# Conv sequence on one core: layer 1's weight steps in three slots, and layer 2's second packed weights made during layer 1

## The chip, the cores and the metric

The kernel runs on one core of a Trainium2 chip. The metric is the device time of one execution in microseconds, as the median of several runs. One execution before was also profiled, and all views below come from it.

## The reference, cut to what matters

Four layers run one after another on a tensor of 16 images, 256 channels and 28 x 28 pixels.

```python
# layer 0: sign of x, 3x3 convolution with sign weights, batch norm, + x
y  = conv3x3(sign(x), sign(w0)) * mean(|w0|);  x = batchnorm(y) + x
# layer 1: 3x3 convolution of signs with real weights, gates, 1x1 convolution, gates
y  = prelu(bn(conv3x3(sign(x), clip(a_w)))); y = bn(gate(y) * y * prelu(x)) + prelu(x)
u  = prelu(bn(conv1x1(sign(y), clip(f_w)))); x = bn(gate(u) * u) + y
# layer 2: two 3x3 convolutions with sign weights, batch norms between and after
h  = prelu(sf1 * conv3x3(sign(batchnorm(x)), sign(w1)), a1)     # sf1 = mean(|w1|)
h  = prelu(sf2 * conv3x3(sign(batchnorm(h)), sign(w2)), a2)     # sf2 = mean(|w2|)
x  = prelu(batchnorm(h) + x, a3)
# layer 3: attention over the 784 pixels of each image, + x
```

The batch norms are over all images. So each convolution with a batch norm behind it has to be finished, statistics included, before the next stage can take its first sign.

## The kernel before, in words

Channels lie on the 128 partitions, in two halves `k`. The work is in stages, and the batch norms part them: layer 0 (up to about 120 us), layer 1 (to about 495 us), the first convolution of layer 2 (to about 604 us, called 2a here), the second (to about 711 us, called 2b), and layer 3.

**Packed sign weights.** Weights of +1 and -1 for two output halves are packed in one fp16 number (`packed_weights`, six chunks). `sign_weights` makes them in six steps: a DMA of 384 KB brings a chunk `st`, ScalarE takes its sign (`sg`, L266) and VectorE packs two halves (`wpk`, L267). `w0` is for layer 0, `w2a` for 2a, and `w2b` for 2b.

**Weight sums.** `weight_sums` brings weights by rows and lets ScalarE sum |w| (L285) and |sign w| (L288), six steps for each layer. `add_up` (L294, L295) ends them on VectorE.

**A step** is a pair of functions: `load` issues the DMA on the SP queue, `work` issues the ScalarE and VectorE work and returns a function for what is to be issued later. `load_ahead(steps, 2)` issues each load two steps before its work.

**`sign_layer`** is the convolution loop of layer 0, 2a and 2b. Within it the order of PE, ScalarE, VectorE and SP is the order in which the program writes it. For each block (an image in layer 0, half an image in layer 2) it issues the matmuls (`products`, L340), the signs of the next image (`sign_image`: L451 in layer 0, L1047 in layer 2), the statistics of the block before (`post`), then one step for each half image, and last the unpacking of this block (`apart`). Unpacking takes the packed sums out of PSUM: ScalarE rounds (L351, L352), VectorE subtracts (L354), and PSUM has three buffers. `post` in layer 0 is `bn_stats` (L588). In layer 2 it is a PReLU and `bn_stats` for each of two channel halves (L1081, L1083), and a square on ScalarE (L1086). The loop that hands out the steps is

```python
for p in range(len(pieces(block))):
    if late:
        late()
    step = steps.pop(0) if first_part(block) + p >= 2 and steps else None
    late = step() if step else None
apart(j)
```

After half image 26 the statistics so far are gathered (`moments.gather`, L167, L168).

**Layer 0's steps** come in rounds of four slots, that is two images, six rounds: `w1_step` (layer 1's weights for one tap row), an empty slot, a step of layer 0's weight sums, a step of `w2a`. `w1_step` clips the weights on VectorE (L501), forms three sums of taps (`asm`, L134), and splits four results in a high part on ScalarE (L510) and a low part on VectorE (L511). The loads share three buffers, tag `x2`.

**Layer 1** is `iteration(b)`, one for each image, about 22 us. Its PE, VectorE and ScalarE order is written out by hand; the order of SP there is the scheduler's. The 3x3 convolution is done as row transforms (`vs`, L134) and matmuls at L686, with sums taken out by L707, L717 and L726; the 1x1 convolution is L796. At the end of iterations 1 to 12 stands one step of the weight sums of `w2a` and `w2b` (`sums12`).

**Between stages** `keep_busy(n)` issues matmuls on zeros (L432). At the end of 2a there are 30 of them, at the end of 2b 45.

**In 2a** the steps of `w2b` take slot 6 and every fourth slot after it, up to slot 26, counted in half images; their loads are issued two steps ahead, the first two at slot 2.

Of the kernel before, what the change touches and what calls it, by code (L numbers as in the profile page):

```python
# [40 lines left out]
B = 16  # L41
# [42 lines left out]
def forward(ctx: ExitStack, tc: tile.TileContext, d: dict, out: bass.AP, careful: bool):  # L84
# [48 lines left out]
    def tt(o, a, b, op):  # L133
        V.tensor_tensor(o, a, b, op)  # L134
        return o
# [112 lines left out]
    def load_ahead(steps, n, now=True):  # L248

        for s in steps[:n] if now else ():  # L250
            s.load()
        return [lambda s=s, t=t: (s.work(), t.load() if t else None)[0] for s, t in zip(steps, steps[n:] + [None] * n)]
# [20 lines left out]
    def weight_sums(room, src, total, at):  # L273


        parts = const.tile([P, 2, 3], F32, name=f"abs_{at}")
        sts = {}

        def load(mo, q):
            st = sts[mo, q] = room()  # L280
            nc.sync.dma_start(out=st, in_=src[mo, :, q * PIECE:(q + 1) * PIECE])

        def work(mo, q):
            st = sts.pop((mo, q))
            A.activation(st, st, AF.Abs, accum_out=parts[:, mo, q:q + 1])  # L285
            if not careful:
                n = at + 3 * mo + q
                A.activation(st, st, AF.Sign, accum_out=nonzero[:, n:n + 1])  # L288
            if (mo, q) == (1, 2):
                return add_up  # L290
            return lambda: None

        def add_up():
            V.tensor_reduce(total, parts, AX.X, ALU.add)  # L294
            V.tensor_scalar(total, total, 1.0 / K9, None, ALU.mult)  # L295

        return [Step(lambda c=c: load(*c), lambda c=c: work(*c)) for c in ((mo, q) for mo in range(2) for q in range(3))]
# [122 lines left out]
    with tc.tile_pool(name="ps_conv", bufs=3, space=PSUM) as psc, \  # L420
# [13 lines left out]
        with tc.tile_pool(name="ph1", bufs=1) as ph:  # L434
# [55 lines left out]
            fw = [ph.tile([P, 2, 256], FR, name=f"fw_{i}") for i in range(2)]  # L490

            def w1_step(k, c):
                sts = []

                def load():
                    sts.append(xpool.tile([P, 3, 256], F32, tag="x2", name="st", bufs=3))
                    nc.sync.dma_start(out=sts[0], in_=d["w1"][k, :, c::3, :])

                def work():
                    st = sts[0]  # L500
                    V.tensor_scalar(st, st, -1.0, 1.0, ALU.max, ALU.min)  # L501
                    t = ph.tile([P, 3, 256], F32, tag="rn", name="asm", bufs=2)
                    a, s, m = (t[:, i, :] for i in range(3))
                    tt(a, st[:, 0, :], st[:, 2, :], ALU.add)
                    tt(s, a, st[:, 1, :], ALU.add)
                    tt(m, a, st[:, 1, :], ALU.subtract)

                    for u, (w, f) in enumerate(((st[:, 0, :], 1.0), (s, 0.5), (m, 0.5), (st[:, 2, :], -1.0))):
                        hi, lo = (x[:, k, c, u, :] for x in w1)
                        A.activation(hi, w, AF.Copy, scale=f)  # L510
                        V.scalar_tensor_tensor(lo, w, f, hi.bitcast(F32), ALU.mult, ALU.subtract)  # L511

                return Step(load, work)

            def fw_step():
                sts = []

                def load():
                    sts.append(xpool.tile([P, 3, 256], F32, tag="x2", name="stf", bufs=3))
                    nc.sync.dma_start(out=sts[0][:, 0:2, :], in_=d["fw"])  # L520

                return Step(load, lambda: split2(fw, sts[0][:, 0:2, :]))
# [45 lines left out]
                    nc.sync.dma_start(out=w_2[64 + 32 * g:65 + 32 * g], in_=d[f"seb2_{q}"])  # L568
                tt(mix_c[:, 1], pv("f_scale"), c2, ALU.mult)

            steps = [w1_step(k, c) for k in range(2) for c in range(3)] + [fw_step()]
            w2a = packed_weights(wpool, tag="wa2")

            def room_sums():
                return xpool.tile([P, PIECE], F32, tag="x2", name="sts", bufs=3)

            signs2, sums0 = sign_weights(xpool, w2a, d["w2a"], ("x2", 3), tmp=ph), weight_sums(room_sums, d["w0_rows"], sf0, 0)
            steps = [s for three in zip(steps, sums0, signs2) for s in three] + steps[6:]
            steps = load_ahead(steps, 2)
            steps[19:19] = [constants]  # L580
            for i in range(6):
                steps[4 * i + 1:4 * i + 1] = [None]

            def post0(block, ab):
                b, r0, rows = block
# [37 lines left out]
            def room_sums():  # L623
                return ph.tile([P, PIECE], F32, tag="sts", name="sts", bufs=2)

            sums12 = weight_sums(room_sums, d["w2a_rows"], sf1, 6) + weight_sums(room_sums, d["w2b_rows"], sf2, 12)

            sums = {}

            def sums_of(t):  # L630
                if t not in sums:
# [207 lines left out]
            def iteration(b):  # L839


                ahead, one, two = b + 1 < B, b >= 1, b >= 2
                if b + 2 < B:
                    xs[b + 2] = None
                    load_x(b + 2, True)
                if b < len(sums12):
                    sums12[b].load()
                for i, u in enumerate((1, 2)):
                    conv_pair(b, 0, i, u)
                if two:  # L850
                    unit_u(b - 2, 0)
                if two:
                    unit_u(b - 2, 1)
                if ahead:
                    enter(b + 1, 0, sc0)
                if one:
                    prelu_y(b - 1, 1)
                if ahead:
                    enter(b + 1, 1, sc0)
                    sign1(b + 1, 0)  # L860
                if two:
                    unit_b(b - 2, 0)
                    unit_b(b - 2, 1)
                sum_pair_a(b, 0)
                conv_pair(b, 0, 0, 0)
                h = hidden_a(b, hidden_x(b)) if one else None
                if ahead:
                    residual_a(b + 1, 0)
                    sign1(b + 1, 1)
                sum_pair_b(b, 0)  # L870
                if one:
                    h = hidden_b(b, h)
                if ahead:
                    residual_a(b + 1, 1)
                    residual_b(b + 1, 0)
                    transform(b + 1, 1)
                    residual_b(b + 1, 1)
                conv_pair(b, 0, 1, 3)
                rows_out(b, 0)
                if one:  # L880
                    g = gates(h)
                else:
                    gate_bias()
                if ahead:
                    transform(b + 1, 2)
                if one:
                    for k in range(2):
                        branch1_a(b - 1, k, g[:, 0])
                for i, u in enumerate((1, 2)):
                    conv_pair(b, 1, i, u)  # L890
                if one:
                    branch1_b(b - 1, 0)
                    branch1_c(b - 1, 0)
                    branch1_b(b - 1, 1)
                prelu_y(b, 0)
                if two:
                    branch2(b - 2, 0, g[:, 1])
                sum_pair_a(b, 1)
                sum_pair_b(b, 1)
                if one:  # L900
                    branch1_c(b - 1, 1)
                if two:
                    branch2(b - 2, 1, g[:, 1])
                    for k in range(2):
                        squares2(b - 2, k)
                if one and b <= len(sums12):
                    sums12[b - 1].work()()
                if ahead:
                    transform(b + 1, 0)
                    transform(b + 1, 3)  # L910
                    for i, u in enumerate((0, 3)):
                        conv_pair(b, 1, i, u)
                    rows_out(b, 1)
                    if one:
                        conv1x1(b - 1)
                else:
                    conv1x1(b - 1)
                    for k in range(2):
                        unit_u(b - 1, k)
                        unit_b(b - 1, k)  # L920
                    for i, u in enumerate((0, 3)):
                        conv_pair(b, 1, i, u)
                    px = hidden_x(B)
                    rows_out(b, 1)
                    prelu_y(b, 1)
                    return px
# [101 lines left out]
        pt = [ppool.tile([P, 2, N], F32, name=f"p_{b}") for b in range(B)]  # L1028

        with tc.tile_pool(name="ph2", bufs=1) as ph:  # L1030
            w2b = packed_weights(ph, tag="wb")
            fpads = sign_pads(ph, "fpads")

            def temp(tag):
# [68 lines left out]
                    while last_squares:  # L1103
                        last_squares.pop(0)()

            steps = sign_weights(xpool, w2b, d["w2b"], ("x2", 3), tmp=ph)

            def first_loads(some=steps[:2]):
                for s in some:
                    s.load()  # L1110

            steps = [first_loads, None] + [t for s in load_ahead(steps, 2, now=False) for t in (None, None, s, None)]
            mom = block_moments("l2b", HALVES)
            sign_layer(fpads, w2a, temp, room2, sign2a, post2(order, pv("a1"), mom, doubts[:, 2 * NB:3 * NB]), steps, mom, HALVES)
            late_squares()
# [601 lines left out]
```

## Time and profile before

| | us |
|---|---|
| median of 3 runs (996.99 to 997.12) | 997.11 |
| the profiled execution's own time | 997.06 |
| its span, first to last instruction | 995.0 |
| PE busy in the span | 961.2 |
| VectorE busy | 799.2 |
| ScalarE busy | 676.3 |
| first matmul of 2a / first matmul of 2b | 495.11 / 605.14 |

The profiled time is 2.06 us more than the span, for what lies around it, and 0.05 us below the median. A busy share is an average over stages with different limits, so it doesn't say what a stage waits for. In the timeline a row is: start, duration, engine, line, operation, tiles, shape, count, and in brackets the idle time before it with what ended it. A row can merge several instructions of one kind. In the table by windows the columns are busy time and count for each engine, then the granted TensorE clock (1.00 is full), the share of DMA time and GB/s.

### The profile page before, as it was taken

How to read it: one execution, taken by the hardware profiler on the slowest of the kernel's cores; microseconds unless marked ns; L12 is line 12 of the kernel's file. 1: busy time of each engine (PE TensorE's matmuls, PEld its weight loads, DVE VectorE, ACT ScalarE, POOL GpSimd, SP SyncE). 2: the span in 40 equal slices, each digit the busy share in tenths (PEclk: the TensorE clock that was granted, in tenths of full speed). 3: DMA queues.
4: the chain of work that ended last, by engine and by line, in shares of the span. 5: the costliest groups of instructions: out<-in, count | busy, mean ns of one | idle time of the engine just before them, and what ended most of it. 6: DMA issues, size and time to landing. Idle time of an engine off the chain costs nothing. (4 is left out here: it accounts for less than half of the span.)

```text
span 995.0 us, 14743 instructions
## 1 busy us (share of the span) xinstructions
PE 961.2 (97%) x5609; PEld 663.4 (67%) x5615; DVE 799.2 (80%) x1416; ACT 676.3 (68%) x1135; POOL 140.9 (14%) x149
## 2 busy tenths in 40 slices
PE   7999899999999999999999998999999999999996
PEld 3555499999999999999555554555444444444442
DVE  4666988999899899996789996999848677777765
ACT  6787436676676666664688876888676767676652
POOL 3000100000000000000100000000053535353521
PEclk9999999999999999999999999999999999999999
DMA  9977512323333322101293100000033343434312
GB/s 346 329 267 251 192 32 80 97 97 120 117 122 120 104 98 82 65 33 64 105 349 130 54 13 1 1 1 1 1 66 62 101 99 97 105 91 113 83 65 101
DMA packets 26949, 105.82 MB, mean 106 GB/s; under 512 B 3491, under 2 KB 7269, under 8 KB 26869
## 3 DMA queue, kind: packets, MB, share of 16 engines
q1 hardware_dynamic: 20948, 73.44, 21.2%
q0 software_dynamic: 5632, 30.54, 11.3%
q8 instruction: 46, 0.75, 0.3%
q10 hardware_dynamic: 288, 0.80, 0.2%
q14 instruction: 35, 0.28, 0.1%
HBM read 72.67 MB, written 32.11 MB: 105 GB/s over the span
## 5 line engine op out<-in xcount | busy, mean ns | idle before, releaser
L340 PE MATMUL cv<-fpads,wpk 128*128 128x392 f16 (+1 forms) x1746 | 297.6, 332 | 14.3 <-ACT fpads L451 5.2
L686 PE MATMUL cv<-vs,w 128*128 128x392 f32 x1536 | 303.0, 355 | 2.8 <-DVE vs L134 2.8
L686 PEld LDWEIGHTS cv<-vs,w 128*128 128x128 f32 x1536 | 288.6, 191 | 4.9 <-issue 3.2
L340 PEld LDWEIGHTS <-wpk 128*128 128x128 f16 x1746 | 169.5, 98 | 142.8 <-issue 13.8
L1296 ACT ACTIVATE es<-sc 128x784 f32<-128x784 f32 x112 | 87.3, 822 | 41.7 <-PE sc L1292 41.7
L1292 PE MATMUL sc<-q,keyswa 64*128 64x392 f32 x448 | 90.0, 513 | 0.9 <-ACT es L1296 0.9
L1081 DVE SCALAR_TENSOR_TENSOR p<-ab,vec 128x392 f32<-128x392 f32 x128 | 79.1, 618 | 2.3
L1313 PE MATMUL av<-es,v 128*64 128x392 f32 x448 | 80.8, 500 | 0.0
L1292 PEld LDWEIGHTS sc<-q,keyswa 64*128 64x128 f32 x448 | 38.9, 186 | 43.9 <-issue 17.1
L1306 POOL TENSOR_TENSOR sum<-sum,es 128x784 f32<-128x784 f32 x32 | 67.2, 2099 | 3.1 <-ACT es L1296 0.6
L134 DVE TENSOR_TENSOR vs<-pad 128x840 fp32r<-128x840 bf16 (+1 forms) x66 | 64.5, 1001 | 0.1
L1313 PEld LDWEIGHTS av<-es,v 128*64 128x64 f32 x448 | 29.4, 136 | 47.3 <-issue 47.0
L824 POOL DMA_DIRECT2D x2d<-x x16 | 8.6, 537 | 359.7 <-DVE x L818 295.1
L1280 DVE COPY keyswa<-mi 64x392 f32<-64x392 f32 x31 | 16.3, 564 | 52.6 <-ACT q L1276 52.5
L707 ACT ACTIVATE t<-cv,c_bn,s_bn 128x392 f32<-128x392 f32 x32 | 21.7, 678 | 49.9 <-PE cv L686 49.9
L351 ACT ACTIVATE t<-cv,rounding 128x392 f32<-128x392 f32 (+2 forms) x82 | 51.4, 627 | 5.2 <-PE cv L340 3.4
L1086 ACT ACTIVATE t<-ab 128x392 f32<-128x392 f32 x64 | 33.5, 523 | 30.0 <-DVE ab L354 30.0
L354 DVE SCALAR_TENSOR_TENSOR ab<-ab,cv 128x392 f32<-128x392 f32 x64 | 35.4, 554 | 20.9 <-ACT ab L352 20.0
L796 PE MATMUL cv<-z,fw 128*128 128x392 f32 x256 | 49.1, 343 | 1.0 <-ACT z L788 0.9
L796 PEld LDWEIGHTS cv<-z,fw 128*128 128x128 f32 x256 | 45.9, 188 | 2.2 <-ACT z L788 2.2
L1269 PE MATMUL mi<-p,wqk 128*128 128x392 f32 x124 | 45.3, 507 | 0.3 <-DVE p L1256 0.3
L1304 POOL TENSOR_TENSOR sum<-es 128x784 f32<-128x784 f32 x16 | 30.0, 1877 | 91.0 <-ACT es L1296 91.0
(284 smaller groups left out, 1459.3 us busy)
## 6 DMA issues: line engine op xcount, KB each, us to landing
xs<-in_x_dram SPq DMA_DIRECT2D x30, 784.0 KB, 4.8
x2d<-x POOLq DMA_DIRECT2D x16, 784.0 KB, 3.6
out_dram<-p SPq DMA_DIRECT2D x15, 784.0 KB, 3.8
p<-x2d POOLq DMA_DIRECT2D x14, 784.0 KB, 6.9
p<-x2d SPq DMA_DIRECT2D x13, 784.0 KB, 8.7
n0d<-n POOLq DMA_DIRECT2D x16, 392.0 KB, 4.9
n<-n0d SPq DMA_DIRECT2D x16, 392.0 KB, 3.1
st<-in_w_dram SPq DMA_DIRECT2D x12, 384.0 KB, 6.2
```

Of the source, the lines that this page charges most:

```text
L134: V.tensor_tensor(o, a, b, op)
L340: T.matmul(pss[j][:, n // size if careful else h, :rows * S].rearrange("p (a b) -> p a b", b=S), lhsT=w[:, n, t, :], rhs=pads[:, blocks[j] ...
L351: A.activation(by_halves(t, blocks[j]), ps, AF.Identity, bias=rounding, scale=1.0 / PACK)
L354: V.scalar_tensor_tensor(a, b, -PACK, ps, ALU.mult, ALU.add)
L686: T.matmul(ps.rearrange("p (a b) -> p a b", b=S), lhsT=w[:, k, c, u, mo * P:(mo + 1) * P], rhs=vs[:, b % 2, u, k, :, c:c + S], start=(n == 0),
L796: T.matmul(ps[:, h, :HN], lhsT=w[:, k, mo * P:(mo + 1) * P], rhs=z2[b][:, k, h * HN:(h + 1) * HN], start=(k + i == 0), stop=(k + i == 2),)
L1081: V.scalar_tensor_tensor(p, y, alpha[:, mo:mo + 1], y, ALU.mult, ALU.max)
L1269: T.matmul(ps[:, h, :HN], lhsT=wqk[:, k, :], rhs=x[b][:, k, h * HN:(h + 1) * HN], start=(k == 0), stop=(k == 1))
L1292: T.matmul(ps[:, h, :HN], lhsT=chunk[rows], rhs=qs[b][rows], start=True, stop=True)
L1296: A.activation(e, ps[:, :, :HN], AF.Exp, scale=0.125)
L1306: (V if late else nc.gpsimd).tensor_tensor(sums[b, late], sums[b, late], e, ALU.add)
L1313: T.matmul(ps[64 * h:64 * h + 64, :HN], lhsT=w, rhs=e[:, h, :], start=start, stop=stop)
```

## The change

In layer 0 the step of layer 1's weights is divided: the clip and the sums of taps stay in their slot, the four high parts go in the slot that was empty, and the four low parts are issued at the start of the slot after that. `load_ahead` now counts only the steps with loads.

In layer 1 the six steps that make `w2b` are put beside the first six steps of the weight sums: in iterations 1 to 6 a sign on ScalarE is issued ahead of that iteration's sums, and the packing on VectorE is issued after `rows_out(b, 1)`, as is the ending of the sums. The loads of both use the two buffers of tag `sts`, and are issued one iteration ahead. `w2b` is moved from the pool of layer 2 to the pool of weights.

2a then has no steps. (`careful` is a second version of the program for inputs that the first can't treat exactly; it runs only where the first leaves a flag, and keeps its old order in layer 2.)

```diff
             def w1_step(k, c):
-                sts = []
+                sts, parts = [], []
...
-                def work():
+                def sums_of_taps():
                     st = sts[0]
                     V.tensor_scalar(st, st, -1.0, 1.0, ALU.max, ALU.min)
                     t = ph.tile([P, 3, 256], F32, tag="rn", name="asm", bufs=2)
...
                     for u, (w, f) in enumerate(((st[:, 0, :], 1.0), (s, 0.5), (m, 0.5), (st[:, 2, :], -1.0))):
-                        hi, lo = (x[:, k, c, u, :] for x in w1)
+                        parts.append((w, f, *(x[:, k, c, u, :] for x in w1)))
+
+                def high():
+                    for w, f, hi, lo in parts:
                         A.activation(hi, w, AF.Copy, scale=f)
+
+                def low():
+                    for w, f, hi, lo in parts:
                         V.scalar_tensor_tensor(lo, w, f, hi.bitcast(F32), ALU.mult, ALU.subtract)
 
-                return Step(load, work)
+                return Step(load, sums_of_taps), high, low
...
-            steps = [w1_step(k, c) for k in range(2) for c in range(3)] + [fw_step()]
...
-            steps = [s for three in zip(steps, sums0, signs2) for s in three] + steps[6:]
-            steps = load_ahead(steps, 2)
-            steps[19:19] = [constants]
-            for i in range(6):
-                steps[4 * i + 1:4 * i + 1] = [None]
+            w1_steps = [w1_step(k, c) for k in range(2) for c in range(3)]
+            ahead = load_ahead([t for s, *three in zip((w for w, _, _ in w1_steps), sums0, signs2) for t in (s, *three)] + [fw_step()], 2)
+            steps = []
+            for (_, high, low), taps, add_up, sign in zip(w1_steps, ahead[0::3], ahead[1::3], ahead[2::3]):
+                steps += [taps, lambda high=high, low=low: (high(), low)[1], add_up, sign]
+            steps += [ahead[-1], constants]
...
+            if not careful:
+                w2b = packed_weights(wpool, tag="wb")
+                signs3 = sign_weights(ph, w2b, d["w2b"], ("sts", 2), sg=("sgb", 1))
...
+            aside = [[]] + [[s] for s in sums12] + [[]] * (B - len(sums12))
+            if not careful:
+                for a, s in zip(aside[1:], signs3):
+                    a.append(s)
...
-                if b < len(sums12):
-                    sums12[b].load()
...
-                if one and b <= len(sums12):
-                    sums12[b - 1].work()()
+                lates = [s.work() for s in aside[b][::-1]]
+                for s in aside[b + 1]:
+                    s.load()
                 if ahead:
                     transform(b + 1, 0)
                     transform(b + 1, 3)
                     for i, u in enumerate((0, 3)):
                         conv_pair(b, 1, i, u)
                     rows_out(b, 1)
+                    for late in lates:
+                        late()
                     if one:
                         conv1x1(b - 1)
...
-            w2b = packed_weights(ph, tag="wb")
+            if careful:
+                w2b = packed_weights(ph, tag="wb")
...
-            steps = sign_weights(xpool, w2b, d["w2b"], ("x2", 3), tmp=ph)
-
-            def first_loads(some=steps[:2]):
-                for s in some:
-                    s.load()
-
-            steps = [first_loads, None] + [t for s in load_ahead(steps, 2, now=False) for t in (None, None, s, None)]
+            steps = []
+            if careful:
...
```

More of the change, by code (lines that the diff above doesn't have):

```diff
@@ L1104, in late_squares, with first_loads @@
                         last_squares.pop(0)()
-            steps = sign_weights(xpool, w2b, d["w2b"], ("x2", 3), tmp=ph)
-            def first_loads(some=steps[:2]):
-                for s in some:
-                    s.load()
-            steps = [first_loads, None] + [t for s in load_ahead(steps, 2, now=False) for t in (None, None, s, None)]
+            steps = []
+            if careful:
+                steps = sign_weights(xpool, w2b, d["w2b"], ("x2", 3), tmp=ph)
+                def first_loads(some=steps[:2]):
+                    for s in some:
+                        s.load()
+                steps = [first_loads, None] + [t for s in load_ahead(steps, 2, now=False) for t in (None, None, s, None)]
             mom = block_moments("l2b", HALVES)
```

## The prediction

> **What bounds the kernel now.** I read the page first (PE is busy for 97% of the span), then the timeline of PE stage by stage, then ScalarE and VectorE where PE has gaps. Busy shares hide the places that matter: at the end of a stage the batch norm waits for the last statistics, and those come from VectorE, not from PE.
>
> Stage 2a first, in the timeline of PE, which the change frees of its steps:
>
> ```profile
> 495.11 92.00 PE L340 MATMUL cv<-fpads,wpk 128*128 128x392 f16 x540 [0.43 <-ACT fpads L1047]
> 588.90 6.28 PE L340 MATMUL cv<-fpads,wpk 128*128 128x392 f16 x36 [1.79 <-DVE ab L354]
> 595.23 6.42 PE L432 MATMUL unused<-idle 128*128 128x512 bf16 x29
> 605.14 7.18 PE L340 MATMUL cv<-fpads,wpk 128*128 128x392 f16 x31 [3.48 <-ACT fpads L1047]
> ```
>
> PE runs without a gap until all three PSUM buffers wait for VectorE (1.79 us). It ends at 595.18, fills with idle matmuls to 601.65, and then stands for 3.48 us. So the stage ends when VectorE ends. One round of four half images between ScalarE and VectorE, from the timeline of 2a:
>
> ```profile
> 555.69 0.83 ACT L266 ACTIVATE sg<-st 128x768 bf16<-128x768 f32 x1
> 557.67 0.56 DVE L354 SCALAR_TENSOR_TENSOR ab<-ab,cv 128x392 f32<-128x392 f32 x1 [0.80 <-ACT ab L352]
> ...
> 560.54 0.54 DVE L267 SCALAR_TENSOR_TENSOR wpk<-sg 128x384 f16<-128x384 bf16 x1
> 561.00 0.56 DVE L354 SCALAR_TENSOR_TENSOR ab<-ab,cv 128x392 f32<-128x392 f32 x1
> ...
> 563.87 0.55 DVE L354 SCALAR_TENSOR_TENSOR ab<-ab,cv 128x392 f32<-128x392 f32 x1
> ...
> 566.73 0.55 DVE L354 SCALAR_TENSOR_TENSOR ab<-ab,cv 128x392 f32<-128x392 f32 x1
> ...
> 570.47 0.56 DVE L354 SCALAR_TENSOR_TENSOR ab<-ab,cv 128x392 f32<-128x392 f32 x1 [0.80 <-ACT ab L352]
> ```
>
> The sign stands ahead of the rounding on ScalarE, and VectorE waits 0.80 us for it; then VectorE pays for the packing. A round takes 570.47 - 557.67 = 12.80 us. PE starts a half image every 3.055 us, or 12.22 a round. Each step puts VectorE 0.58 us further behind. Stage 2b is the same loop without steps, and is the measure of what 2a can be. I took the distance from the end of half image 26's last matmul to its L354: 583.27 - 577.88 = **5.39 us** in 2a, and 691.31 - 689.55 = **1.76 us** in 2b. In 2b it is 1.76 or 1.58 in every half image from 2 to 26; in 2a it is so from 2 to 5, before the first step, and then grows.
>
> Stage 2b starts slowly. The granted clock, in windows of 2 us:
>
> ```profile
> 606.00:608.00 2.00, 2.00 (x10) 0.95 (x9) 0.00 (x0) 2.00 (x4) 0.00 (x0) 0.64 0.00 0
> 608.00:610.00 2.00, 2.00 (x8) 0.91 (x7) 0.00 (x0) 0.74 (x1) 0.00 (x0) 0.50 0.03 8
> ```
>
> The clock is at half for 3.41 us from 606.58. Half image 0 takes 4.97 us, 3.33 in 2a; from then on 2b is 1.64 us later in its stage than 2a was.
>
> Layer 0, one round of two images: an image with `w1_step`, then the next.
>
> ```profile
> 61.52 0.54 DVE L267 SCALAR_TENSOR_TENSOR wpk<-sg 128x384 f16<-128x384 bf16 x1
> 61.98 0.55 DVE L501 TENSOR_SCALAR st<-st 128x768 f32<-128x768 f32 x1
> 62.57 0.42 ACT L510 ACTIVATE w<-st 128x256 fp32r<-128x256 f32 x1 [2.48 <-DVE st L501]
> ...
> 66.36 0.97 DVE L354 SCALAR_TENSOR_TENSOR n<-n,cv 128x784 int16<-128x784 int16 x1 [1.23 <-ACT n L352]
> ...
> 72.16 0.97 DVE L354 SCALAR_TENSOR_TENSOR n<-n,cv 128x784 int16<-128x784 int16 x1 [2.82 <-ACT n L352]
> ```
>
> ScalarE is the bound here. It waits 2.48 us for the clip, because the clip stands behind the statistics of the image before. PE gets its signs late, 1.14 us in a round of 13.54.
>
> Layer 1, iteration 6 of ScalarE and VectorE:
>
> ```profile
> 258.32 0.68 ACT L707 ACTIVATE t<-cv,c_bn,s_bn 128x392 f32<-128x392 f32 x1 [2.72 <-PE cv L686]
> 259.03 0.62 DVE L717 SCALAR_TENSOR_TENSOR uvs<-cv,s_bn,t 128x392 f32<-128x392 f32 x1 [1.17 <-ACT t L707]
> ```
>
> Both wait for PE once in each iteration, and PE (100% busy in every window from 140 to 460) waits for neither.
>
> [...] one drop lasts 3.41 us and follows the 3.48 us gap; another follows a gap of 2.78 us at layer 1's start; gaps of 1.14 us (layer 0) and 1.79 us (2a) have none. [...] In this trace a 384 KB load took 3.3 to 4.0 us from 51 to 84 us, and up to 7.7 in the crowded stretch from 42 to 47.
>
> **The change, part by part.**
>
> *2a loses six signs and six packings.* With no steps 2a should keep 2b's 1.76 us. At half image 26 that is 5.39 - 1.76 = 3.63 us. At half image 27, after the gathering, the last packing is gone too: L354 follows L354 after 5.01 us in 2a and 4.55 in 2b, so 0.46. Half images 28 to 31 are equal (2.86 us each in both). Sum: **4.09 us** off the end of 2a. Next in line is PE's pace, with L354 at its natural distance; PE would no longer stand 1.79 us. The six loads of `w2b` in 2a go as well, so the loads of `p` run without them between; half images 2 to 5 keep 2b's distances even in the crowded stretch, so that is worth nothing.
>
> *2b starts warm.* PE's real work in 2a ends at 595.18 less the gap (1.95 us from start to start at half image 30), so 593.2; with 6.47 us of idle matmuls, 599.7. The first sign of 2b allows PE at 605.14 - 4.09 = 601.05. The gap is then about **1.35 us** instead of 3.48. Gaps up to 1.79 us left the clock alone, so I take the drop as gone: 1.64 us more. Bounds: 0 and 1.64.
>
> *Layer 1 gets the six signs (0.83 us) and six packings (0.54 us), 8.2 us of engine work.* The sign stands ahead of the sums at an iteration's end. Queued behind it are `unit_u` (L809, at 252.51 at once after the sums), which moves to about 253.25, the next `unit_u` and the next sign; behind these ScalarE waits 2.72 us for PE, so 0.75 us is absorbed. VectorE reads `u` at 255.47, later than 254.2. The PSUM buffer that `unit_u` frees is wanted by PE only at about 258.2. The packing stands behind `rows_out(b, 1)`, which is what PE waits for first in the next iteration (ended 252.69, wanted 253.56), so it doesn't delay that. It delays `enter` and four PReLUs by 0.5 us, absorbed in the 1.17 us wait; `hid` needs its sums 2.5 us after they are ready. In iterations 6 and 12 `add_up` no longer stands in front of the transforms (VectorE waited 1.94 us for it at 273.62); PE hadn't waited there, so nothing. On SP the new load follows the sums' load and stands ahead of the `n` load, which is held by VectorE until 255.6; the new load can go at about 253.3. Cost **0**; if the cover is gone, 1.37 us x 6 = 8.2 at most, 0.54 x 6 = 3.2 if only the packing shows.
>
> *Layer 0.* The built program's queues show ScalarE with the same order as before, and VectorE with the low parts (1.42 us) moved from before L354 of one image to before L354 of the next. In the first they stood ahead of a wait of 1.23 us, in the second ahead of one of 2.82. Neither wait is VectorE's own, so nothing is gained and 1.40 us of cover remain. The wait of 2.48 us stays: clip and statistics keep their order. What changes is a load: buffers are freed later, and the next taps' load waits for ScalarE's |sign| of the sums instead of the low parts. It goes at 56.1 instead of 51.62. Loads issued there landed in 3.3 us, so at 59.4 to 60, wanted at 61.98. The tightest is the second, issued at 42.6 and landing by my count at 46 to 47.2, wanted at 48.44. Cost **0**. If ScalarE were freed, the gain is bounded by PE's gaps after 50 us: 0.80 + 3 x 1.14 + 0.77 = 5.0 us.
>
> *Sum:* 997.06 - 4.09 - 1.64 = 991.33, against the profiled execution's own time; the median stands 0.05 above that, so **991.4**.
>
> **The rivals.** (a) *The clock still drops at 2b's start:* 997.1 - 4.1 = 993.0. [...] against: 1.35 us is shorter than a gap that left the clock alone. (b) *Layer 1 shows the packings:* 991.4 + 3.2 = 994.6; VectorE is over 90% busy there, but it waits 1.17 us after the place. (c) *Layer 0 is freed as the split suggests,* up to 5.0 us: 986.4. Against it is ScalarE's unchanged order. (d) *Slower: the taps' loads arrive late.* If all five took the 7.6 us of the crowded stretch, each would land at 63.7 instead of 61.98 and hold clip, ScalarE and PE for 1.7 us: 8.7 us, so 1000.1. It decides from 5.9 us on, and turns the sign from 5.9 + 5.7 / 5 = 7.0. The measured 3.3 to 4.0 speak against it. (e) *Nothing moves,* because 2a's end is set by something that steps don't touch: 997.1. Against: the distance grows exactly with the steps.
>
> **How the numbers follow.** My forecast 0.70, (a) 0.13, (b) 0.06, (c) 0.03, (d) 0.05, (e) 0.03. The range goes from 989.8 (layer 1's start, with a clock drop after 2.78 us, may lose or keep it: 1.6) to 994.0, which takes in (a) and part of (b). A measurement of this kernel tells about 0.2%, 2 us, from no change: faster 0.91, same 0.04, slower 0.05.
>
> **What would show it.** Right: L354 of half image 26 in 2a 1.8 us behind PE, no 1.79 us gap, a gap of 1 to 1.5 us ahead of 2b with clock 1.00, 2a to 2b 105.9 us apart, first matmul of 2a still at 495.1. Wrong: a wait of the clip for a DMA in layer 0, PE gaps at L686, or the 2a distance still growing.

## The result, and the profile after

| | before | after |
|---|---|---|
| median, us | 997.11 (996.75 to 998.53, 5 runs) | 992.97 (990.84 to 993.37, 5 runs) |
| ratio | | 0.9955, interval 0.9943 to 0.9967 |
| profiled execution, its own time / span | 997.06 / 995.0 | 991.88 / 989.8 |
| first matmul of layer 1 to first matmul of 2a | 371.41 | 369.83 |
| first matmul of 2a to first matmul of 2b | 110.03 | 105.94 |
| first matmul of 2b to first matmul of layer 3 | 109.69 | 108.04 |
| last matmul for the flag (L1401 before, L1418 after) to issue of the last store | 3.54 | 4.60 |
| landing of the last store | 3.45 | 4.63 |

The kernel is 4.1 us faster by the medians, inside the range and 1.6 us above the forecast. The table holds all that moved by over 0.1 us between the two profiled executions: -1.58 - 4.09 - 1.65 + 1.06 + 1.18 = -5.08, of a span that is 5.18 shorter. Two of these terms were in the forecast sum, the one of 4.09 to the last digit. The first was only allowed for in the range, and the last two were not forecast. The experiments have to say what belongs to the change and what to this one execution.

The timeline of PE after the change, 2a and the start of 2b:

```profile
493.45 98.05 PE L340 MATMUL cv<-fpads,wpk 128*128 128x392 f16 x576 [0.43 <-ACT fpads L1062]
591.56 6.42 PE L432 MATMUL unused<-idle 128*128 128x512 bf16 x29
599.39 20.82 PE L340 MATMUL cv<-fpads,wpk 128*128 128x392 f16 x121 [1.41 <-ACT fpads L1062]
```

All 576 matmuls of 2a are now one row: the wait of 1.79 us for L354 is gone. The gap ahead of 2b is 1.41 us, where 1.35 was worked out. VectorE in the round that the prediction showed (lines of PReLUs and statistics left out):

```profile
553.54 0.56 DVE L354 SCALAR_TENSOR_TENSOR ab<-ab,cv 128x392 f32<-128x392 f32 x1 [0.30 <-ACT ab L352]
...
556.42 0.54 DVE L354 SCALAR_TENSOR_TENSOR ab<-ab,cv 128x392 f32<-128x392 f32 x1
...
559.65 0.56 DVE L354 SCALAR_TENSOR_TENSOR ab<-ab,cv 128x392 f32<-128x392 f32 x1 [0.30 <-ACT ab L352]
...
562.52 0.55 DVE L354 SCALAR_TENSOR_TENSOR ab<-ab,cv 128x392 f32<-128x392 f32 x1
...
565.77 0.56 DVE L354 SCALAR_TENSOR_TENSOR ab<-ab,cv 128x392 f32<-128x392 f32 x1 [0.30 <-ACT ab L352]
```

A round takes 565.77 - 553.54 = 12.23 us, which is PE's pace, where it took 12.80. The distance from half image 26's last matmul, which ends at 576.23, to its L354 at 577.98 is 1.75 us, where it was 5.39. The windows at the start of 2b and at the end of the kernel (columns as before: the clock is the third from the right):

```profile
600.00:602.00 2.00, 2.00 (x13) 1.17 (x12) 0.00 (x0) 2.00 (x4) 0.00 (x0) 1.00 0.00 0
602.00:604.00 2.00, 2.00 (x14) 1.14 (x12) 0.00 (x0) 1.97 (x4) 0.00 (x0) 1.00 0.03 8
...
978.00:980.00 2.00, 1.26 (x8) 1.18 (x10) 0.77 (x5) 0.00 (x0) 0.00 (x0) 0.73 0.00 0
980.00:982.00 2.00, 1.92 (x12) 1.40 (x10) 1.30 (x4) 0.00 (x0) 0.00 (x0) 0.50 0.06 16
```

2b starts at full clock. But the clock is at half from 978.91, under the last matmuls of layer 3. The end of the kernel in the timeline of PE, of before:

```profile
985.66 0.19 PE L1401 MATMUL mi<-turned,ok 128*1 128x1 f32 x2 [1.68 <-DVE ok L1400]
986.35 0.60 PE L1373 MATMUL mi<-o,wp 64*128 64x196 f32 x4 [0.50 <-DVE flag L1402]
```

and of after:

```profile
978.24 0.19 PE L1418 MATMUL mi<-turned,ok 128*1 128x1 f32 x2 [1.68 <-DVE ok L1417]
978.93 1.03 PE L1390 MATMUL mi<-o,wp 64*128 64x196 f32 x4 [0.50 <-DVE flag L1419]
```

The gaps are the same, 1.68 and 0.50 us with a matmul of 0.19 between; after the change the clock falls right after the second gap, and the same four matmuls take 1.03 us instead of 0.60.

Layer 0 after, ScalarE and VectorE in the round that was shown of before:

```profile
62.34 0.42 ACT L512 ACTIVATE w<-st 128x256 fp32r<-128x256 f32 x1 [2.48 <-DVE st L501]
...
66.13 0.97 DVE L354 SCALAR_TENSOR_TENSOR n<-n,cv 128x784 int16<-128x784 int16 x1 [2.57 <-ACT n L352]
...
71.93 0.97 DVE L354 SCALAR_TENSOR_TENSOR n<-n,cv 128x784 int16<-128x784 int16 x1 [1.50 <-ACT n L352]
```

ScalarE waits the same 2.48 us for the clip. VectorE's two waits have changed places, as the low parts moved from one image to the next: 1.23 became 2.57 and 2.82 became 1.50. Layer 1 after, iteration 6:

```profile
256.81 0.68 ACT L720 ACTIVATE t<-cv,c_bn,s_bn 128x392 f32<-128x392 f32 x1 [2.36 <-PE cv L699]
257.52 0.62 DVE L730 SCALAR_TENSOR_TENSOR uvs<-cv,s_bn,t 128x392 f32<-128x392 f32 x1 [0.71 <-ACT t L720]
```

ScalarE's wait fell from 2.72 to 2.36 us and VectorE's from 1.17 to 0.71: of the added work at least 0.36 and 0.46 us lie in these waits. PE works through an iteration in 21.95 us (from 236.93 to 258.88, two starts of L618), as in before (238.44 to 260.39, L613).

### The profile page after: what moved, and what is told of

Read it like the earlier page. It is cut to its first block, busy times and chain, and to the rows that moved or that the text cites. A ratio compares the mean times of both kernels' runs of the same rounds, so it can differ in the third digit from the quotient of the medians.

```text
span 989.8 us, 14752 instructions
## 1 busy us (share of the span) xinstructions
PE 959.3 (97%) x5609; PEld 662.7 (67%) x5615; DVE 799.7 (81%) x1416; ACT 676.6 (68%) x1135; POOL 140.9 (14%) x149
## 4 chain that ended last, share of the span: by engine, by line
PE 45%; DVE 4%; ACT 1%; issue 1%; DVEq 0%; ACTq 0%
PE cv L340 19%; PE sc L1309 8%; PE av L1330 8%; PE mi L1286 4%; PE sm L1372 2%; PE mi L1390 2%; PE sm L1330 1%; DVE p L1096 1%; DVE r L1356 1%; DVE ab L354 0%; DVE l2c_fin L1098 0%; DVE l2b_fin L1098 0%; DVE p L1273 0%; PE sc L1390 0%; DVE p L1272 0%
## 5 line engine op out<-in xcount | busy, mean ns | idle before, releaser
L720 ACT ACTIVATE t<-cv,c_bn,s_bn 128x392 f32<-128x392 f32 x32 | 21.7, 678 | 49.9 <-PE cv L699 49.9
L354 DVE SCALAR_TENSOR_TENSOR ab<-ab,cv 128x392 f32<-128x392 f32 x64 | 35.4, 554 | 17.6 <-ACT ab L352 17.6
```

The source lines that it names most:

```text
L354: V.scalar_tensor_tensor(a, b, -PACK, ps, ALU.mult, ALU.add)
```

## The experiments

A run of one kernel scatters with a standard deviation of about 1.1 us (35 runs of before lie from 994.8 to 999.5), so effects of about 1 us are read from the traces, and the times only support them. The changed kernel has 11 runs in all, with a mean of 992.5; before has a mean of 996.9.

### 1 and 2. Each half of the change alone

The first kernel is before with the edits of layer 0 alone (three functions and the three slots), the second is the changed kernel with layer 0 as before.

> The kernel before with the layer 0 part of the change alone. Theory (ScalarE's order is unchanged, its wait of 2.48 us for the clip stays): no change, 997.1, within 0.5; PE gaps of 1.14 us a round stay, first matmul of 2a at 495.1 or, if layer 1's start keeps its clock in that execution, 493.5. Rival (the split frees ScalarE): up to 5.0 us less, 992.1. Rival (late taps' loads): up to 8.7 us more, with the clip waiting for a DMA.

> The changed kernel with layer 0 as before: only the making of w2b is moved to layer 1. Theory: all of the gain is here, so the changed kernel's time, 991 to 993.4; distance from 2a's first to 2b's first matmul 105.9 us, from 2b's to layer 3's 108.0. Rival (layer 0 gave part of it): 994 to 997.

Measured: layer 0 alone 996.60 us against 996.86, ratio 0.9995 (0.9985 to 1.0005). The `w2b` part alone 992.23, ratio 0.9948 (0.9934 to 0.9961). PE in the round shown of before:

```profile
67.13 12.40 PE L340 MATMUL cv<-fpads,wpk 128*128 128x392 f16 x72 [1.14 <-ACT fpads L451]
```

Layer 0 alone in the timeline of ScalarE:

```profile
62.27 0.42 ACT L512 ACTIVATE w<-st 128x256 fp32r<-128x256 f32 x1 [2.48 <-DVE st L501]
```

and of PE:

```profile
66.83 12.40 PE L340 MATMUL cv<-fpads,wpk 128*128 128x392 f16 x72 [1.14 <-ACT fpads L451]
```

So a round is still 12.40 + 1.14 = 13.54 us, and layer 0's part of the change is worth nothing that shows. The late loads of rival (d) are refuted with it: ScalarE's waits for the clip add up to 14.4 us over the six steps in before, in this kernel and in the changed one, and VectorE is idle ahead of no clip. The gain is the move of `w2b`: that part alone has a mean of 992.2, the changed kernel 992.5. PE with that part alone:

```profile
495.56 98.05 PE L340 MATMUL cv<-fpads,wpk 128*128 128x392 f16 x576 [0.43 <-ACT fpads L1057]
...
601.52 23.71 PE L340 MATMUL cv<-fpads,wpk 128*128 128x392 f16 x138 [1.43 <-ACT fpads L1057]
```

2a to 2b is 105.96 us and 2b 108.05, as in the changed kernel. Layer 1 took 371.30 us here, as before, with a clock drop at its start (124.99). So the 1.58 us that the changed kernel's profiled execution gained in layer 1 are no part of the change: in that execution the clock just didn't fall there (it is full from 6.11 to 978.91 us). With a drop at its start layer 1 takes 371.40 to 371.42 us in the three traces with the old place of `w2b`, and 371.19 to 371.30 in five traces with the new one.

### 3. Before, with only 2b's start kept warm

```diff
-            keep_busy(30)
+            keep_busy(45)
```

> The kernel before with 45 idle matmuls in place of 30 at 2a's end, so that PE's gap ahead of 2b is about 0.3 us and not 3.48; the steps stay in 2a. Theory (the gap alone costs 2b 1.64 us through the clock): 995.5, 2a to 2b still 110.0 us, 2b to layer 3 108.0 instead of 109.7. Rival (2b's slow start has another cause, such as the order of the signs): 997.1, 109.7.

Measured: 996.47 us, ratio 0.9993 (0.9985 to 1.0002); the means of 22 and 35 runs differ by 0.67 us with a standard error of 0.39. PE:

```profile
596.14 9.87 PE L432 MATMUL unused<-idle 128*128 128x512 bf16 x45
606.26 14.03 PE L340 MATMUL cv<-fpads,wpk 128*128 128x392 f16 x81 [0.24 <-ACT fpads L1047]
```

The gap is 0.24 us, the drop is gone, and 2b takes 108.06 us instead of 109.69. 2a keeps its 110.05 us: the 1.64 us are separate from the 4.09, as the sum has them. But the mean times show only 0.67 of them.

### 4 and 5. The changed kernel with 2b cold again, and the changed kernel once more

```diff
-            keep_busy(30)
+            keep_busy(20)
```

> The changed kernel with 20 idle matmuls in place of 30 at the end of 2a, so that PE's gap ahead of 2b is 3.5 us again, as it was before the change. Theory (a gap of 1.41 us keeps the clock, one of 3.5 us loses it): a drop at 2b's start, 2b to layer 3 109.7 us instead of 108.05, 2a to 2b unchanged at 105.9; 1.6 us more than the changed kernel beside it, about 994. Rival (the time of 2b's start doesn't reach the end, as the run with 45 idle matmuls in the old kernel showed only 0.4 us): less than 0.7 us more.

> The changed kernel once more, beside the run with the cold start of 2b. Theory: 991.5 to 993.4, 2a to 2b 105.9, 2b to layer 3 108.05; from the last flag's matmul to the last store's issue 4.0 to 4.6 us if the clock drops there, 3.5 if not. Rival (the end is not tied to the clock): 4.6 us without a drop.

Measured: 993.09 us cold (ratio 0.9962, 0.995 to 0.9975) and 992.55 unchanged (0.9958, 0.9945 to 0.9972). PE in the cold kernel:

```profile
593.92 4.26 PE L432 MATMUL unused<-idle 128*128 128x512 bf16 x19
601.78 10.41 PE L340 MATMUL cv<-fpads,wpk 128*128 128x392 f16 x50 [3.59 <-ACT fpads L1062]
```

With the gap at 3.59 us the drop comes back (603.23), and 2b takes 109.70 us; in the repeat it takes 108.06. In the traces the step is 1.64 us, in the mean times 0.6 with a standard error of 0.57. Together with the experiment before: 2b is at 109.7 in all three traces with a cold start and at 108.04 to 108.07 in all nine with a warm one, while the times show some 0.65 us of it. Where the rest goes in executions without a trace stays open. The mean granted clock of the runs helps only in part. Over the 22 runs of experiment 3 it is 0.9962 against 0.9939 over the 35 of before, where one drop of 3.41 us at half clock makes 0.0017 of a span of 995 us; but in ten of the 22 it is 0.993 to 0.995, no higher than in before, and these have a mean of 997.4 us against 995.3 of the other twelve. Over the cold runs of experiment 4 and those of experiment 5 it is the same, 0.9945. So drops at other places, which come in some executions only, weigh about as much in this mean, which also counts those behind the last matmul (in the trace of before from 992.28 us on): the trace of experiment 5 has one at 10.41 us that no other trace has.

### 6. The changed kernel with layer 1's start kept warm

```diff
-            keep_busy(28)
+            keep_busy(40)
```

> The changed kernel with 40 idle matmuls in place of 28 at the end of layer 0, so that PE's gap ahead of layer 1 is about 0.4 us and not 2.95. Theory (the changed kernel's runs between 990.8 and 993.4 are those with and without a clock drop at layer 1's start, 1.65 us, and near the end, 1.06 us): the upper runs go, so a median of 991 to 992 and a spread under 2 us; 2a's first matmul at 493.5 in every execution. Rival (the spread is in the last stores, or the drop is elsewhere): median 993, spread as before.

Measured: 990.65 us, ratio 0.9932 (0.9918 to 0.9946). The runs still lie 2.7 us apart, where under 2 was expected, and 2a starts at 494.20 us in the trace, where 493.5 was. PE:

```profile
114.29 8.80 PE L432 MATMUL unused<-idle 128*128 128x512 bf16 x40
...
124.34 5.92 PE L699 MATMUL cv<-vs,w 128*128 128x392 f32 x30 [1.26 <-DVE vs L134]
```

No drop at the start, and layer 1 takes 369.86 us: the value of the changed kernel's profiled execution, which had a gap of 2.95 us (2.78 before) and happened to be spared. Its second trace (the repeat above) has the drop at 126.47 and 371.21 us. The drop at layer 1's start is therefore one that comes or not. It costs 371.21 - 369.83 = 1.38 us in the changed kernel.

### 7. The changed kernel with the end kept warm

```diff
         A.copy(os[b][0], avs[b][:, :HN])
+        keep_busy(7)
         up = raise_flag(two_banks(psmi, "mi")[:, 0, :])
```

> The changed kernel with seven idle matmuls ahead of the last flag's matmul, in PE's last gap of 1.68 us. Theory (the last outputs were matmuls at half clock, which cost 1.06 us of the gain in the changed kernel's trace): from the flag's matmul to the last store's issue 3.5 us instead of 4.6, no clock drop there; 1 us less than the changed kernel's time on average. Rival (the last store's landing, 4.6 us instead of 3.4, is what gives the gain back, and has nothing to do with PE): the landing stays at 4.4 to 4.6.

Measured: 991.48 us, ratio 0.9947 (0.9934 to 0.9961), 0.7 us below the changed kernel by the means. PE:

```profile
977.90 1.68 PE L1279 MATMUL sm<-idle 128*128 128x512 bf16 x7
979.64 0.19 PE L1418 MATMUL mi<-turned,ok 128*1 128x1 f32 x2
980.33 0.60 PE L1390 MATMUL mi<-o,wp 64*128 64x196 f32 x4 [0.50 <-DVE flag L1419]
```

With the wait of 1.68 us filled, the last matmuls take 0.60 us again, the flag's matmul stands 3.54 us ahead of the last store's issue, and the store lands in 3.42 us. Both terms at the end are gone with the clock drop. Over the traces: in the seven with the short 2a and an unfilled end the first stretch is 3.55 to 4.61 us, 4.16 in the mean, and the landing 3.36 to 4.63, 3.88 in the mean; in the three with the old 2a they are 3.54 and 3.44 to 3.45 each time. So the end takes back (4.16 - 3.54) + (3.88 - 3.45) = 1.05 us in the mean of the traces. With three traces on one side, this doesn't show that the shorter 2a brings the drop.

### 8. The high parts one slot later

In the changed kernel ScalarE still meets the high parts behind the clip of the same image. Here they come one slot later, after the step of the weight sums:

```diff
-                steps += [taps, lambda high=high, low=low: (high(), low)[1], add_up, sign]
+                steps += [taps, add_up, lambda high=high, low=low: (high(), low)[1], sign]
```

> The changed kernel with the slots of layer 0 in the order taps, weight sums, high parts, signs: the high parts move to the next image, away from the clip that they wait for. Theory (ScalarE's wait for the clip, 2.48 + 0.50 us a round, is what makes PE wait 1.14 us a round; that wait is what the change left in place): no wait of the high parts for the clip, PE gaps in layer 0 go, up to 5.0 us less, so layer 0's last matmul near 110 instead of 114.6 and a time of 987 to 989. Rival (the loads bound layer 0, or VectorE does): the wait goes but the PE gaps stay, or the next taps come late; no gain.

Measured: 985.54 us, ratio 0.988 (0.9865 to 0.9895). The end of layer 0 on PE in the changed kernel:

```profile
112.92 1.71 PE L340 MATMUL cv<-fpads,wpk 128*128 128x196 f16 x18 [0.80 <-DVE n L354]
```

and here:

```profile
15.66 91.97 PE L340 MATMUL cv<-fpads,wpk 128*128 128x392 f16 x558 [0.17 <-ACT fpads L451]
...
117.24 8.98 PE L699 MATMUL cv<-vs,w 128*128 128x392 f32 x39 [3.56 <-DVE vs L134]
```

and ScalarE:

```profile
61.87 1.59 ACT L451 ACTIVATE fpads<-xs 128x784 f16<-128x784 f32 x2
63.36 0.40 ACT L512 ACTIVATE w<-st 128x256 fp32r<-128x256 f32 x1
```

The wait for the clip is gone, because ScalarE signs the next image first. From 15.66 us on the timeline lists no gap of PE in layer 0, and its last matmul ends at 107.64 us instead of 114.63: 7.0 us, which is also the difference of the mean times (985.5 against 992.5).

### 9. Four packings instead of one in layer 1

In iterations 1 to 6 the packing is issued four times, from the same signs into the same tile.

```diff
                     for late in lates:
-                        late()
+                        for _ in range(4 if 1 <= b <= 6 and late is lates[0] else 1):
+                            late()
```

> The changed kernel with the packing of w2b on VectorE issued four times over in iterations 1 to 6 of layer 1 (the same result, 1.6 us more of VectorE in each). Theory (one packing is covered by VectorE's wait of 1.17 us; four, 2.2 us, fill more than is free): VectorE falls behind, and layer 1 is 1 to 4 us longer, with PE gaps at the 3x3 matmuls. Rival (there is no cover, the single packing already showed): 6 x 1.6 = 9.7 us more. Rival (cover is ample): nothing, less than 0.3 us.

Measured: 993.86 us, ratio 0.9967 (0.9956 to 0.9979), 1.5 us over the changed kernel by the means. Layer 1 takes 373.93 us instead of 371.21. PE, from one iteration to the next:

```profile
239.66 0.61 PE L618 MATMUL hid<-g,se 128*128 128x2 f32 x4 [0.25 <-DVE g L134]
...
262.13 0.61 PE L618 MATMUL hid<-g,se 128*128 128x2 f32 x4 [0.25 <-DVE g L134]
```

PE now waits for VectorE, and this iteration takes 22.47 us instead of 21.95. Three more packings are 3 x 0.54 = 1.62 us of VectorE in an iteration, and 2.72 / 6 = 0.45 us show in the mean. So some 1.17 us were free after the change. VectorE's wait of 0.71 us for L720 is one part of it; that the rest is time in which PE didn't need VectorE yet follows only by subtraction. The first packing was covered, with room for two more.

### 10. The three edits together

The edits of experiments 6, 7 and 8 in one kernel.

> The changed kernel with the order of slots of the run before the last, 40 idle matmuls ahead of layer 1, and seven ahead of the last flag. Theory: the gains add, 5.0 in layer 0, up to 1.65 at layer 1's start where the clock dropped, 1.06 at the end: 985 to 987. Rival (layer 0 gives nothing): 990.

Measured: 982.92 us (982.12 to 983.37), ratio 0.9856 (0.9841 to 0.9871). PE at layer 1's start:

```profile
107.69 8.80 PE L432 MATMUL unused<-idle 128*128 128x512 bf16 x40
...
117.02 8.21 PE L699 MATMUL cv<-vs,w 128*128 128x392 f32 x42 [0.53 <-DVE vs L134]
```

Layer 1 takes 369.82 us, the end 3.54 and 3.40. The clock is full until 978.39 us, after the last matmul. It beats both kernels, before by 14 us and the changed one by 10; of these 7 are the move of the high parts, where 5.0 was put in, and so it lies 2 us below the expected range.

## Why the prediction was right

**2a, -4.09:** right in cause and size. The distance of L354 from PE was the whole cost of the steps, and the loop without steps in 2b gave what it would be without them.

**2b starts warm, -1.64:** right in the traces (-1.65), with the gap at 1.41 us. Rival (a), a drop that stays, is refuted for the traces. In the times only a part is found, and that is open.

**Layer 1, 0:** right. Rival (b) is refuted: one packing takes 0.54 us, and experiment 9 found room for that and two more. The two iterations in which `add_up` moved out of the way, 6 and 12, even became 0.08 us shorter (22.03 to 21.95), where nothing was expected.

**Layer 0, 0:** right. Rival (c) was rightly given little, for the reason named: ScalarE's order didn't change. But its size was wrong. The bound of 5.0 us added the gaps that the timeline lists as waits for the signs; it left out the last one, 0.80 us for L354, and the short ones that the timeline doesn't list. From 15.92 us on, PE takes 98.95 us for 558 matmuls in before; the same 558 take 98.93 in the changed kernel and 91.97 in experiment 8. That is 7.0 us, of which listed gaps make 5.8. Rival (d) had less against it than was said. The 384 KB load of `w2a` at 71.45 us took 6.52 us, more than the 3.3 to 4.0 named for that stretch and more than the 5.9 from which (d) decides; its full price is 5 x 1.72 = 8.6 us, not 8.7. Rival (e) is refuted by 2a's length.

**The sum** is 1.6 us too low against the medians, which is within the range. It has no term for the end of the kernel, with its waits of 1.68 and 0.50 us. In the profile of before they cost only themselves. In five of the seven traces with the short 2a a clock drop met the last matmuls early (in a sixth only the last few), for 1.05 us in the mean of the seven. Two sums then fit the means of the runs, where 992.5 was measured with a standard error of 0.3. With the traces' values, 996.9 - 4.09 - 1.65 + 1.05 = 992.2. With the 0.65 us that the times show for 2b's start, and the end equal in both kernels, 996.9 - 4.09 - 0.65 = 992.2 too. The record doesn't decide between them. The end of before is spared in its three traces, but in 16 of the 35 runs of before the mean clock is 0.993, where the traced execution has 0.995: by the 0.0017 above half clock for about one drop more, at a place that isn't known. The allowance of 1.6 us for layer 1's start was right: the drop there was missing in the changed kernel's first trace and there in its second.

## What to carry to other kernels

Where a stage ends with statistics on an engine other than PE, follow the distance between that engine and PE through the stage: if it grows with each extra step, the steps are paid in full although PE is 97% busy, and a loop without them is the measure. When work is moved off a stage, look at every idle stretch of PE later on, also where nothing is edited, since a clock drop may come or go there (here one that cost 1.65 us went at 2b's start, and in some traces one came at the end). A step that is divided helps only if the waiting engine gets other work ahead of its second half: with the same order nothing came, and one slot later it was 7 us.

## What was not expected of the hardware

Two gaps with a matmul of 0.19 us between them (1.68 + 0.50 us) were followed by half clock in the changed kernel's end; a single gap of 1.79 us in 2a of before was not. At layer 1's start a gap of 2.78 us was followed by a drop in before, at 125.30 us, and one of 2.95 us in the changed kernel's first trace was not. Over the twelve traces:

| where | PE's gap, us | traces | with a drop |
|---|---|---|---|
| layer 1's start | 2.78 to 4.20 | 10 | 9 |
| layer 1's start, kept warm | 0.53 and 1.26 | 2 | 0 |
| 2b's start | 3.48 to 3.59 | 3 | 3 |
| 2b's start, with the short 2a or kept warm | 0.24 to 1.44 in seven of them | 9 | 0 |
| the end, up to the last matmul | 1.68 + 0.50 | 10 | 6 |

So the length of a gap alone doesn't settle whether the clock falls: the same 1.68 + 0.50 us had a drop in six traces and none in four, and 2.95 us had none where 2.78 us had one. What else decides, the record doesn't show, and no experiment tested it.

The last store landed in 4.28 to 4.63 us in the three traces in which the clock fell within a microsecond of the flag's matmul, and in 3.36 to 3.70 us in the nine others. Filling the end with matmuls took both away together: the two traces with it are among the nine, with 3.42 and 3.40 us. What links a transfer to the clock of TensorE, no run here shows.
